# A planned order of work is drawn again: scatters ask later for their turn, and chance decides near ties

## The chip, the cores and the metric

The kernel runs on one core of a Trainium2 chip. A core has five engines, each with its own queue of instructions that it works off in order: TensorE (PE in the profile, PEld for its weight loads), VectorE (DVE), ScalarE (ACT), GpSimd (POOL) and SyncE (SP), which here only issues transfers. Engines wait for each other by semaphores. The metric is the device time of one execution in microseconds. Before the change it was 1603.57 us, the median of seven runs between 1598.36 and 1611.09.

## The reference

The input is x, 128 sequences of 32 tokens of width 256, and a context of 257 rows of width 256 for each sequence. Two layers are computed, each an addition to x after a layernorm:

```python
x = x + L0_xattn(layernorm(x), ctx)   # one head, all 257 context rows
x = x + L0_attn(layernorm(x))         # causal over the 32 tokens, one head of 128
x = x + L0_ffn(layernorm(x))          # 256 -> 1024 -> 256, ternary weights, 8-bit activations
x = x + L1_xattn(layernorm(x), ctx)   # 16 heads of 16
x = x + L1_attn(layernorm(x))         # five neighbours of each token
x = x + L1_ffn(layernorm(x))          # 8 experts 256 -> 1024 -> 256, two per token, with a capacity
```

For the last step each token's two best experts are found, the tokens are put into the experts' slots, each expert computes its slots, and the results are added to x, weighted by the two gates. A token that finds its expert full gets nothing from it.

## The kernel before

The 4096 tokens are 32 groups of 128 tokens (four sequences). A group goes through the first five steps and the choice of experts in `router` (L1123) as one thread of work; six groups are under way at a time, each in a lane of buffers. At the end of `router` the group's x is stored to the output and its normed rows to a table in HBM, each by one transfer that POOL issues (L1125 and L1128). After some groups a round of routing (`route`, L1166) finds ranks and slots for their tokens, and scatters token numbers and gates into a table of slots.

The experts' work is cut into 72 tiles of 128 slots (`expert_tile`, L1396). For each tile POOL issues four gathers (L1149): the first and second weight matrix of the expert (1 MB each, `w`, `kT` or `kn` by the buffer that is free), the slots' token numbers and gates (`ids`), and the tokens' rows (`xt`). PE turns the rows (L1433), does the two products (L373, with `xTm` and with `hT`), ACT does gelu between them (L1455), and ACT or DVE multiplies by the gate into `y` (L1474, L1475). Then POOL issues a scatter that adds `y` to the output (L1154). There are two buffers for `y`, and each is given back only when its scatter is done. The tiles of the early rounds run among the groups; some two dozen are left when the last group is through, and make the tail of the kernel.

The order of the instructions is not written by hand. Class `Order` (L80 to L229) is a small planner that runs while the kernel is built. Every thread is a generator that yields what it needs next: a buffer from a set (`Slots`), a pause in nanoseconds, another thread's end, or a list with an engine, a length in nanoseconds and the function that emits the instructions. `go_on` (L128) advances a thread until it asks for an engine, and puts it among the ready ones. `run` (L186) takes, again and again, the ready step that could begin first by the planner's own clock; among equal ones the thread's rank decides, which is mostly the number of the group. The emitted order is what each engine's queue then holds on the chip. In places where the planner foresees PE idle for at least 220 ns and little work in the time just before, `idle` (L477) puts in fillers, matmuls of the identity and a matrix of ones whose result nobody reads.

Three locks, each a set with one item, keep the planner from ordering transfers to the same table side by side: `at_slots`, `at_rows` and `at_out`. `locked` (L1141) is what takes them. It is called by the 72 scatters of `y` and the 32 stores of x with `at_out`, by the stores of normed rows with `at_rows`, and by the scatters of token numbers with `at_slots`; two transfers that clear spare rows of the output also use `at_out`. A thread gets the lock, then pauses for `EARLY`, 2500 ns, so that the data is surely there when POOL comes to the instruction, then asks for the engine, and gives the lock back when the planner's time for the landing, `LAND`, 4000 ns, is over. For a scatter of `y` that takes POOL for 1620 ns of the planner's time, so the lock is held for 2500 + 1620 + 4000 = 8120 ns. These numbers are the planner's, not measured ones.

Of the kernel before, what the change touches and what calls it, by code (L numbers as in the profile page):

```python
# [1 line left out]

# [66 lines left out]
class Slots:  # L69


    def __init__(self, items):
        self.free = [(0.0, i, t) for i, t in enumerate(items)]
        self.waiting = []
# [10 lines left out]
class Order:  # L85
# [5 lines left out]

    LAG = {"PE": 300.0, "DVE": 130.0, "ACT": 150.0, "POOL": 90.0, "SP": 3500.0}
    TABLE = 1300.0
    SWITCH = 1000.0
# [1 line left out]

    def __init__(self):
        self.until = dict.fromkeys(self.LAG, 0.0)  # L100
        self.idle = lambda ns: None
        self.recent = []
        self.array = 0.0
        self.ready = []
        self.table = None
        self.parts = None
        self.now = None
# [20 lines left out]
    def go_on(self, t, value):  # L128

        while True:  # L130
            try:
                ask = t.work.send(value)
            except StopIteration:
                t.done = t.at
                for w in t.waiting:
                    w.at = max(w.at, t.at)
                    outer, self.now = self.now, w
                    self.go_on(w, None)
                    self.now = outer
                return  # L140
            value = None
            if isinstance(ask, Slots):
                if not ask.free:
                    ask.waiting.append(t)
                    return
                best = min(ask.free, key=lambda f: f[:2])
                ask.free.remove(best)
                t.at = max(t.at, best[0])
                value = best[2]
            elif isinstance(ask, float):  # L150
                t.at += ask
            elif not isinstance(ask, list):
                if ask.done is None:
                    ask.waiting.append(t)
                    return
                t.at = max(t.at, ask.done)
            else:
                t.ask = ask
                self.ready.append(t)
                return  # L160

# [24 lines left out]
    def run(self):  # L186
        while self.ready:
            best = None
            for t in self.ready:
                for choice in t.ask:  # L190
                    begin = max(t.at, self.until[choice[0]])
                    ns = choice[1]
                    if choice[0] != "PE" and len(choice) > 3 and choice[3] and choice[3] != self.table:
                        ns += self.TABLE
                        begin += self.SWITCH
                    elif choice[0] == "PE" and self.divided(choice) != self.parts:
                        ns += self.DIVIDE if self.divided(choice) else self.WHOLE
                        begin += self.UNDIVIDED if self.divided(choice) else self.UNWHOLE
                    key = (begin, t.rank, begin + ns)
                    if best is None or key < best[0]:  # L200
                        best = (key, t, choice, ns)

            t = best[1]
            choice, ns = best[2], best[3]
            if len(t.ask) > 1:
                ends = [max(t.at, self.until[c[0]]) + c[1] + self.SPARE.get(c[0], 0.0) for c in t.ask]
                choice = t.ask[ends.index(min(ends))]
                ns = choice[1]
            self.ready.remove(t)
            if choice[0] == "PE":  # L210
                if self.divided(choice) != self.parts:
                    ns = choice[1] + (self.DIVIDE if self.divided(choice) else self.WHOLE)
                self.parts = self.divided(choice)
            elif len(choice) > 3 and choice[3]:
                self.table = choice[3]
            begin = max(t.at, self.until[choice[0]])
            if choice[0] == "PE":
                self.keep_busy(begin)
            array = self.array
            choice[2]()  # L220
            if choice[0] == "PE":
                self.recent.append((begin, begin + ns, self.array - array))
            self.until[choice[0]] = begin + ns
            t.at = begin + ns + (choice[4] if len(choice) > 4 else self.LAG[choice[0]])
            t.ask = None
            outer, self.now = self.now, t
            self.go_on(t, None)
            self.now = outer
        self.span = max(self.until.values())  # L229
# [3 lines left out]
def perceiver(ctx: ExitStack, tc: tile.TileContext, a: dict, out: bass.AP):  # L233
# [163 lines left out]
    at_slots, at_rows, at_out = (Slots([None]) for _ in range(3))  # L397
# [123 lines left out]
    def transfer(kb, emit):  # L521
        return [("SP", max(450.0, 1024 * kb / RATE), emit, None, 0.0)]

    def load_context(bs, got):

        kTs, kns = [], []
        for b in bs:
            kTs.append((yield from taken_from(keysT)))
            yield transfer(257, lambda: nc.sync.dma_start(kTs[-1][0], a["ctxT"][b]))
        for b in bs:  # L530
            kns.append((yield from taken_from(keys)))
            yield transfer(256, lambda: nc.sync.dma_start(kns[-1][0], a["ctx"][b]))
        got += zip(kTs, kns)
# [589 lines left out]
    def router(g, ln):  # L1123
        xg = ln.x
        sent = [order.thread(locked(at_out, "POOL", 1000, lambda: nc.gpsimd.dma_start(out[g * P : (g + 1) * P, :], xg)), order.now.rank)]  # L1125
        xn = yield from layernorm(ln, xg)
        sent.append(
            order.thread(locked(at_rows, "POOL", 1000, lambda: nc.gpsimd.dma_start(x_rows[g * P : (g + 1) * P, :], xn)), order.now.rank)  # L1128
        )
        xT = yield from transposed(ln, xn, "xnT")  # L1130
        ps = yield ps_g
        yield pe(430, lambda: products(ps[:, 0:E], [(xT[:, kc, :], wr[:, kc, :]) for kc in range(2)]))
        yield dve(75, lambda: nc.vector.tensor_copy(logits[:, g, :], ps[:, 0:E]))
        order.give(ps_g, ps)
        for t in sent:
            yield t

    EARLY = 2500.0
    LAND = 4000.0

    def locked(lock, engine, ns, emit):  # L1141

        yield lock
        yield EARLY
        yield [(engine, ns, emit, None, LAND)]
        order.give(lock, None)

# [18 lines left out]
    def route(r):  # L1166
# [103 lines left out]
        for i in range(RB):  # L1270
            for k in range(2):
                yield from locked(
                    at_slots, "POOL", 1000, lambda: scatter(slot_ids, islot[:, k, i : i + 1], ids[:, k, i, :])
                )
# [208 lines left out]
    def loads(*pairs):  # L1483
        for dst, src in pairs:
# [3 lines left out]
            yield transfer(n / 1024, lambda: nc.sync.dma_start(dst, src))  # L1488
        yield order.LAG["SP"]

# [172 lines left out]
    def load_one(b, kv):  # L1663
        yield from load_context([b], kv)
        yield order.LAG["SP"]

# [146 lines left out]
```

## Time and profile before

| what | value |
|---|---|
| median of seven runs | 1603.57 us |
| profiled execution | 1614.34 us, of which span 1612.6 us |
| mean granted clock of TensorE | 0.973 of full speed |
| matmuls on PE | 93% of the span busy |
| ACT, DVE, POOL | 62%, 61%, 48% busy |
| moved by DMA | 336.39 MB, 209 GB/s in the mean |
| the scatters of `y` | 72, POOL busy 1.63 us for each, from 422.7 us to the end |

The span runs from the first to the last instruction. Busy time counts instructions that compute or, on POOL, issue a transfer; waiting is not busy. A row of a timeline gives the start, the length, the engine, the line in the kernel, the operation, what is written and read, how many were merged into the row, and in brackets how long the engine was idle before it and who ended that. One matmul of 32-bit numbers in the program is two records in the trace.

### The profile page before, as it was taken

Reading aid. Unit: us, or ns where it says so; the run is one execution under the profiler, and the core shown is the slowest. Engines: PE = TensorE matmul, PEld = TensorE weight load, DVE = VectorE, ACT = ScalarE, POOL = GpSimd, SP = SyncE. Lnnn points to the kernel's source line nnn. Section 1 sums busy time; section 2 is a strip of 40 time slices with the busy share of each in tenths; the row PEclk is TensorE's granted clock in tenths of the full one; section 3 lists DMA queues with packets and bytes.
Section 4 is the critical chain, followed back from the end, with each engine's and each line's share of the span. In section 5 each row is a group of like instructions: output and inputs, shape, how many; then the busy total and the mean of one; then the engine's idle time right before and its main releaser. Section 6 shows DMA issues by size and latency. Waiting matters only on the chain. (4 is left out here: it accounts for less than half of the span.)

```text
span 1612.6 us, 43426 instructions
## 1 busy us (share of the span) xinstructions
PE 1494.6 (93%) x16758; PEld 1234.2 (77%) x16758; DVE 984.8 (61%) x3547; ACT 1003.3 (62%) x2654; POOL 775.4 (48%) x1025
## 2 busy tenths in 40 slices
PE   7889889798899999999999999999999999999997
PEld 6666666567667787887888788778877788888897
DVE  3777768887977777668566865777766744320000
ACT  1467756676767767777777676868777665322221
POOL 3412213344245555444445546445544556677763
PEclk8999989899999999999999999999999999999999
DMA  8673356356246676666666666757574367789996
GB/s 299 200 240 118 102 162 210 94 165 227 77 150 239 205 272 194 224 195 212 232 211 229 216 218 232 243 179 240 166 253 163 127 207 235 243 272 303 293 309 188
DMA packets 133150, 336.39 MB, mean 209 GB/s; under 512 B 17744, under 2 KB 43344, under 8 KB 114256
## 3 DMA queue, kind: packets, MB, share of 16 engines
q0 software_dynamic: 41984, 179.40, 34.2%
q1 hardware_dynamic: 90816, 154.09, 29.5%
q8 instruction: 132, 2.16, 0.6%
q14 instruction: 74, 0.61, 0.1%
q10 hardware_dynamic: 144, 0.13, 0.0%
HBM read 309.68 MB, written 23.87 MB: 207 GB/s over the span
## 5 line engine op out<-in xcount | busy, mean ns | idle before, releaser
L990 ACT ACTIVATE probs<-sps,nm 128x256 f32<-128x256 f32 x512 | 240.5, 485 | 44.1 <-DVE nm L946 35.3
L545 POOL TENSOR_SCALAR rstd<-mv 128x1 f32<-128x1 f32 x192 | 49.9, 260 | 427.1 <-DVE mv L540 344.2
L373 PE MATMUL ps<-w,hT 128*128 128x256 f32 x832 | 219.8, 389 | 2.8 <-DVE mx L707 1.4
L373 PE MATMUL ps<-xTm,w 128*128 128x128 f32 x1504 | 202.6, 278 | 0.9 <-ACT wide L509 0.4
L373 PEld LDWEIGHTS ps<-xTm,w 128*128 128x128 f32 x1504 | 190.0, 192 | 14.6 <-issue 3.6
L608 PE MATMUL sps<-ident,probs 128*128 128x128 f32 x1024 | 155.9, 287 | 18.4 <-ACT probs L990 16.0
L944 DVE TENSOR_REDUCE nm<-sps 128x2 f32<-128x512 f32 x256 | 164.0, 683 | 13.9 <-PE sps L373 13.9
L373 PEld LDWEIGHTS ps<-w,hT 128*128 128x128 f32 x832 | 147.2, 193 | 27.9 <-issue 7.6
L509 ACT COPY probsT<-sps 128x512 f32<-128x512 f32 x242 | 138.8, 595 | 46.3 <-PE sps L608 44.4
L1455 ACT ACTIVATE hT<-ps 128x512 f32<-128x512 f32 x144 | 85.4, 597 | 130.9 <-PE ps L373 128.6
L608 PEld LDWEIGHTS sps<-ident,probs 128*128 128x128 f32 x1024 | 122.9, 148 | 39.0 <-ACT probs L990 30.9
L1149 POOL DMA_INDIRECT w<-in_w_moe,i_exp x99 | 100.9, 1019 | 99.3 <-PE ps L373 59.4
L1154 POOL DMA_INDIRECT out<-y,ids x72 | 117.1, 1627 | 52.2 <-issue 25.3
L546 POOL TENSOR_TENSOR rstd<-rstd,mhalf 128x1 f32<-128x1 f32 x192 | 112.1, 584 | 16.1
L509 ACT COPY xnT<-ps 128x256 f32<-128x256 f32 x174 | 64.2, 376 | 80.6 <-PE ps L560 75.8
L990 ACT ACTIVATION_READ_ACCUMULATOR probs<-sps,nm 128x1 f32 x512 | 110.1, 215 | 0.0
L549 DVE TENSOR_SCALAR xn<-x,mv,rstd 128x256 f32<-128x256 f32 x173 | 73.6, 425 | 45.6 <-POOL rstd L546 44.3
L1154 POOL DMA_INDIRECT slot_ids<-tok_ids,islot x64 | 67.2, 1050 | 52.5 <-DMA slot_ids<-tok_ids,islot 20.4
L560 PE MATMUL ps<-ident,xn 128*128 128x128 f32 x384 | 76.1, 286 | 17.1 <-DVE xn L549 6.8
L373 PEld LDWEIGHTS sps<-probsT,kn 128*32 128x32 f32 x4096 | 67.3, 112 | 27.8 <-issue 16.3
L373 PE MATMUL sps<-probsT,kn 128*32 128x64 f32 x4096 | 85.6, 225 | 2.9 <-ACT probsT L509 2.6
L1475 ACT ACTIVATE y<-ps,ids 128x256 f32<-128x256 f32 x71 | 33.7, 475 | 85.5 <-PE ps L373 58.2
(304 smaller groups left out, 3531.5 us busy)
## 6 DMA issues: line engine op xcount, KB each, us to landing
kT<-in_ctxT SPq DMA_DIRECT2D x256, 257.0 KB
kn<-in_ctx SPq DMA_DIRECT2D x256, 256.0 KB
x<-in_x SPq DMA_DIRECT2D x32, 128.0 KB
last<-in_ctx_last SPq DMA_DIRECT2D x32, 128.0 KB
out<-x POOLq DMA_DIRECT2D x32, 128.0 KB
x_rows<-xn POOLq DMA_DIRECT2D x32, 128.0 KB
x_rows<-nothing SPq DMA_DIRECT2D x7, 512.0 KB
w<-in_w SPq DMA_DIRECT2D x2, 1024.0 KB
```

Source lines behind the costliest of these rows:

```text
L373: nc.tensor.matmul(out, lhsT=lhsT, rhs=rhs, **how)
L509: ("ACT", 60 + 0.815 * n, lambda: nc.scalar.copy(out, in_)),
L545: nc.gpsimd.tensor_scalar(rstd, mv[:, 1:2], EPS, None, ALU.add)
L546: nc.gpsimd.tensor_tensor(rstd, rstd, mhalf, ALU.pow)
L549: yield either(326, 1250, lambda e: e.tensor_scalar(xn, xg, mv[:, 0:1], rstd, ALU.subtract, ALU.mult))
L560: nc.tensor.transpose(pt[:, c, :], x[:, c * P : (c + 1) * P], ident)
L608: nc.tensor.transpose(by_key[:, i, c, :], e[:, i * LK + c * P : i * LK + (c + 1) * P], ident)
L944: nc.vector.tensor_reduce(nm[:, :, r], sps[r].rearrange("p (j k) -> p j k", j=2), AX.X, ALU.max)
L990: lambda: nc.scalar.activation(e[:, (2 * i + j) * LK : (2 * i + j + 1) * LK], sps[r][:, j * LK : (j + 1) * LK], AF.Exp, bias=nm[:, j, r : ...
L1149: nc.gpsimd.indirect_dma_start(out=dst, out_offset=None, in_=src, in_offset=bass.IndirectOffsetOnAxis(ap=idx, axis=0))
L1154: nc.gpsimd.indirect_dma_start(out=dst, out_offset=bass.IndirectOffsetOnAxis(ap=idx, axis=0), in_=src, in_offset=None, compute_op=op)
L1455: yield act(495, lambda: nc.scalar.activation(hT[:, 4 * half : 4 * half + 4, :].rearrange("p f t -> p (f t)"), hps, AF.Gelu), "gelu")
```

## The change

Three edits. The first is in `locked`: for `at_out` alone, the pause `EARLY` now comes ahead of the lock, so a scatter or a store of x waits out its slack while another holds the lock, and the planner holds the lock 2500 ns shorter. The other two are in the planner. Each time a thread asks for an engine, it gets a `late` between 0 and 80 ns from a random generator with a fixed seed, and `run` adds it to the time at which the step could begin when it compares the ready steps. The time at which the planner then lets the step begin is as before. With the fixed seed the order is the same in each build.

```diff
+    SEED, NOISE = 92, 80.0
...
     def __init__(self):
         self.until = dict.fromkeys(self.LAG, 0.0)
+        self.chance = random.Random(self.SEED)
...
                 t.ask = ask
+                t.late = self.NOISE * self.chance.random()
                 self.ready.append(t)
                 return
...
                 for choice in t.ask:
-                    begin = max(t.at, self.until[choice[0]])
+                    begin = max(t.at + t.late, self.until[choice[0]])
...
     def locked(lock, engine, ns, emit):
 
-        yield lock
-        yield EARLY
+        if lock is at_out:
+            yield EARLY
+            yield lock
+        else:
+            yield lock
+            yield EARLY
         yield [(engine, ns, emit, None, LAND)]
         order.give(lock, None)
```

## The prediction

> **What bounds the kernel now.** I read the page first, then busy time by stage, then the waits of the last stage, then single rows in order of time. The profiled execution took 1614.34 us (span 1612.6 us and 1.7 us around it), 10.8 us above the median of the seven runs, 1603.57 us. I make the sum against 1614.34 and carry the difference over to the median.
>
> ```profile
> PE 1494.6 (93%) x16758; PEld 1234.2 (77%) x16758; DVE 984.8 (61%) x3547; ACT 1003.3 (62%) x2654; POOL 775.4 (48%) x1025
> ```
>
> TensorE has work for 93% of the span. No instruction of real work is added or removed by this change, so time can only move where PE is idle, slow or doing filler. The second view is busy time by stage (after the length: PE, PEld, DVE, ACT, POOL, each with its count, then granted clock, DMA share, GB/s).
>
> ```profile
> 0.00:520.00 520.00, 448.40 (x5596) 339.65 (x5597) 387.35 (x1342) 324.35 (x953) 177.04 (x320) 0.94 0.54 174
> 520.00:1080.00 560.00, 544.85 (x6481) 453.73 (x6480) 390.31 (x1396) 412.25 (x1069) 280.61 (x367) 0.99 0.68 221
> 1080.00:1360.00 280.00, 267.96 (x3101) 225.59 (x3100) 178.09 (x654) 196.67 (x497) 153.46 (x183) 0.99 0.61 197
> 1360.00:1412.00 52.00, 50.66 (x360) 46.04 (x359) 19.17 (x103) 19.32 (x36) 34.40 (x40) 1.00 0.72 225
> 1412.00:1525.00 113.00, 105.27 (x705) 97.20 (x705) 9.85 (x56) 29.81 (x57) 81.17 (x76) 0.98 0.89 288
> 1525.00:1612.00 87.00, 77.42 (x526) 71.96 (x524) 0.00 (x0) 20.92 (x42) 48.73 (x43) 0.98 0.82 257
> ```
>
> Read the first number after the length: PE idles 71.6 us up to 520, 27.2 us from there to 1360 (15.1 and 12.0), and in the tail of expert tiles 1.3 and 7.7 us; the last 9.6 us are mostly the final scatter and the end. The tail is where the scatters matter. Its rows in order of time (start, length, engine, line, in brackets the idle time before and who ended it):
>
> ```profile
> 1482.57 1.62 POOL L1154 DMA_INDIRECT out<-y,ids  x1 [0.30 <-ACT hT L1455]
> ...
> 1490.86 0.47 ACT L1475 ACTIVATE y<-ps,ids 128x256 f32<-128x256 f32 x1 [2.41 <-DMA out<-y,ids]
> ...
> 1491.39 1.13 PE L373 MATMUL ps<-kT,hT 128*128 128x256 f32 x4 [0.77 <-ACT y L1475]
> 1491.48 0.61 ACT L1455 ACTIVATE hT<-ps 128x512 f32<-128x512 f32 x1
> 1491.55 1.61 POOL L1154 DMA_INDIRECT out<-y,ids  x1 [2.33 <-ACT y L1475]
> ...
> 1498.50 1.60 POOL L1154 DMA_INDIRECT out<-y,ids  x1 [0.30 <-issue]
> ...
> 1510.73 1.13 PE L373 MATMUL ps<-xTm,kT 128*128 128x128 f32 x8 [2.50 <-DMA kT<-in_w_moe,i_exp]
> 1511.70 1.43 PE L373 MATMUL ps<-w,hT 128*128 128x256 f32 x4
> 1512.93 1.92 PE L373 MATMUL ps<-xTm,kT 128*128 128x128 f32 x8
> 1514.63 1.51 PE L373 MATMUL ps<-w,hT 128*128 128x256 f32 x4
> 1515.98 1.06 PE L373 MATMUL ps<-xTm,kT 128*128 128x128 f32 x8
> ```
>
> This is one story. The y scattered at 1482.57 was begun at 1472.71 and ended at 1473.19: the scatter stood 9.4 us behind its result. It let go of its buffer 8.3 us after its start (the y two tiles on waits for it until 1490.86). Two y buffers turn over in two tiles, and a PE tile takes 4 x 0.89 + 4 x 0.865 + 0.22 = 7.24 us here (rows of 8, 4 and 2 matmuls between neighbours), so 14.5 us; 9.4 + 8.3 = 17.7 is too long. The next y is late, PE waits 0.77, POOL stands 2.33 in front of a scatter with weight gathers behind it, and two tiles later PE waits 2.50 us for weights and then runs slow until about 1516. POOL cannot catch up: from 1491.55 to 1498.50 a scatter and four gathers stand back to back and take 6.95 us of every 7.24.
>
> **The change part by part.** The order in which both programs were built can be compared without a run.
>
> *The scatters.* In the tail of before, a scatter of tile k stands behind the second weight gather of tile k+3 (30 scatters) and late on behind the row gather of k+5; in the changed order, for the last 22 full steps, behind those of k+2 and mostly k+4. One POOL instruction of 1.6 us moves ahead of two gathers of 1.25 us (0.95 and a gap of 0.30): 2.5 us earlier, so a lag of 6.9 and a turnover of 15.2 instead of 17.7 us. What it adds: the scatter meets its wait for y earlier, and behind it on POOL are the gathers of two weights, ids and rows. Hidden while the lag stays positive; it was 4.2 to 9.4 us from 1467 to 1597. The waits the story explains are, in the tail, kT 3.1, kn 1.2 and y 0.8 us, and 1.8 us of slow rows (1.43 for 1.03, 1.92 for 1.05, 1.51 for 1.03): 6.9. Ends: all PE waits of the tail (9.8) and the slow rows, a gain of 11.6; or five scatters that each hold POOL 2.5 us too early, less the 0.29 us that POOL has spare in each of 24 tiles, a loss of 5.5. I take -7, since the lag left is nearer to the rows with slack. The 32 stores of the groups' x go through the same function; each is one POOL instruction of 0.66 us that no PE step waits for: 0.
>
> *The fillers.* Both programs put matmuls of ones into foreseen idle time of PE. Before has 65, of which 24 (48 rows) stand between 1382 and 1429; the changed order has 44, none there.
>
> ```profile
> 1382.41 1.81 PE L373 MATMUL sps<-ident,ones 128*128 128x128 f32 x14
> 1384.05 0.38 PE L560 MATMUL ps<-ident,xn 128*128 128x128 f32 x2
> 1384.27 0.61 PE L373 MATMUL sps<-ident,ones 128*128 128x128 f32 x4
> ```
>
> No wait follows here: the next real step was ready and stood behind 1.64 and 0.62 us of filler. With the groups at 1386, 1397, 1425 and 1427 (0.40, 0.22, 0.68, 0.67) that is 4.2 us; a last group of 14 is followed by a wait of 2.27 us and costs nothing. I take -4, ends -4.2 and +1.8: with the filler gone the wait at 1425 may be 2.27 + 1.6 = 3.9 us, and the row at 1510 shows what follows a wait of 2.50 us, matmuls that lose 1.8 us; the granted clock from 1500 to 1520 is 0.91. One rule speaks against this part. The Trainium skill (TensorE: Matmul & The Clock Gate, Part 1) says that an idle window of about 3.4 us halves the clock, and by its figures a window at half clock would cost 1.7 us, an estimate near the trace's, though the trace's threshold lies lower.
>
> *The chance.* Up to 80 ns on a step's readiness changes who goes first, and from there on the whole order. Three things can be counted. (a) Changes between matmuls of the whole array and of parts of it: 438 before, 468 after. From 701.86 two rows of 0.112 take 0.32 until the first matmul on parts, and coming back eight take 1.00 instead of 0.89: 0.1 us each, 30 x 0.1 = +3 (0 if they fall into idle time, 4.5 at half as much again). (b) The first loads: the second folding weight is now the fifth load of SP, not the third, behind two x tiles of 128 KB; at 298 GB/s (first 40 us) +0.9 us. The weights now interleaved with the first group's context put its last keys at about 5.0 MB / 298 GB/s = 17 us and 2 to 3 for landing; they are used at 21.61: hidden, 2 us to spare. (c) Steps whose chain from the last PE product, at mean row lengths, is longer than the PE work ordered between: 113 with 35.7 us short before, 132 with 42.8 after (24.1 to 26.0 in the stage to 520; 9.0 to 13.9 to 1360). That is 7 us more, but chains explain only 36 of 108 us of idle PE; the rest is waiting behind other work on ACT and DVE, which the order alone doesn't price. Scaled to the real idle time it would be 5.6 + 14.8 + 1.5 = 22. On the other side the idle share that chains don't explain could fall by a tenth of its 72 us, -7. Fillers outside the tail, 41 and 44, say that the planner foresees as much idle time as before. I take 0, ends -7 and +22.
>
> Sum: -7 - 4 + 3 + 1 + 0 = -7, so 1614.3 - 7 = 1607.3 us profiled, and 1603.57 - 7 = 1596.6, say 1597 us.
>
> **Rivals.** *Same time.* The tail is as much DMA as PE: share 0.89 and 288 GB/s up to 1525, and 24 tiles instead of 23 follow the last routing. If weights arrive no sooner, -7 becomes 0 and fillers pay for mode changes: -4 + 3 + 1 = 0, 1604. Against it: the rows above show a late issue, not a slow transfer. *Slower by the groups' stages.* The tighter chains between 520 and 1360 cost what the scaling says, +14.8: -7 + 14.8 = +8, 1611. It decides from 7 us of idle PE added there. For it: 36 tight steps become 52; against: DVE and ACT are at 70 and 74% from 520 to 1080, so queues are not full, and another ready step usually covers. *Slower by blocked gathers.* Scatters wait at POOL's head for y: +5.5 for -7, -4 + 3 + 1 + 5.5 = 5.5, 1609; from three such waits on. Against: lags of 4 to 9 us. That the order isn't changed as said is excluded by the built order.
>
> **How the numbers follow.** Forecast 0.50, same time 0.20, groups' stages 0.21, blocked gathers 0.09. About 0.3% (4.8 us) is what a measurement can tell from no change. The forecast's own range, 1583 to 1602, has a sixteenth within that bound; same time gives most of its chance to it: faster 0.49, same 0.21, slower 0.30. Range: 1603.6 - 11.6 - 4.2 - 7 + 1 = 1582 below, and the two slower cases with a little over, 1614 above.
>
> **What would show it.** In the profile after: no filler between the last two routings; waits of y for the DMA of out gone from ACT in the tail, and scatters 4 to 7 us behind y; PE's waits for kT and kn in the tail under 2 us and no rows of 1.9 us. PE idle from 80 to 1360 within 5 us of 84; more means that the chance costs what I set to nothing. I am wrong if POOL waits for y ahead of many scatters, or if stages before 1360 shift by over 8 us either way.

## The result, and the profile after

The changed kernel takes 1612.74 us (median of 31 runs, 1607.22 to 1618.31), before 1605.06 us (73 runs, 1596.20 to 1615.53). The ratio is 1.0048, with a 95% interval of 1.0037 to 1.0060: **slower by 7.7 us**, where the forecast was faster by 7. It lies inside the range given, and near the rival that loses in the groups' stages (1611 us).

One caution first. The profiled execution of before was a long one (1614.34 us, 9 us over the median), that of the changed kernel (1613.55 us) is 0.8 us over its own. So the two pages show equally long kernels, and the loss can't be read from them by subtraction. Further down I use profiles of other kernels that hold before's order.

The page and the busy time by stage of the changed kernel (after the length: PE, PEld, DVE, ACT, POOL, then granted clock, DMA share, GB/s):

```profile
PE 1494.1 (93%) x16716; PEld 1228.2 (76%) x16716; DVE 992.1 (62%) x3566; ACT 997.6 (62%) x2637; POOL 774.0 (48%) x1024
```

```profile
0.00:520.00 520.00, 450.10 (x5537) 342.45 (x5538) 393.42 (x1351) 320.13 (x939) 167.62 (x312) 0.93 0.55 176
520.00:1080.00 560.00, 543.01 (x6481) 448.41 (x6483) 387.00 (x1364) 411.95 (x1068) 288.70 (x374) 1.00 0.66 214
1080.00:1360.00 280.00, 268.89 (x3153) 223.61 (x3146) 187.50 (x707) 196.97 (x497) 150.67 (x184) 1.00 0.62 205
1360.00:1412.00 52.00, 49.15 (x324) 45.88 (x323) 16.16 (x100) 18.68 (x35) 36.81 (x40) 0.93 0.76 242
1412.00:1525.00 113.00, 108.35 (x742) 100.78 (x741) 7.97 (x46) 30.37 (x60) 84.03 (x78) 1.00 0.92 295
1525.00:1612.00 87.00, 74.56 (x492) 67.07 (x491) 0.00 (x0) 19.52 (x40) 46.12 (x41) 0.97 0.78 249
```

PE is idle for 69.9 us up to 520, for 28.1 from there to 1360 and for 19.9 after that; before had 71.6, 27.2 and 18.6. Idle time alone shows next to nothing. The waits of PE in the tail, from 1410 on (us in total, times, longest):

```profile
PE ps L378 <- DMA kT<-in_w_moe,i_exp: 5.1, 5, 1.8
PE ps L378 <- DMA w<-in_w_moe,i_exp: 3.1, 4, 1.6
PE ps L378 <- DMA kn<-in_w_moe,i_exp: 0.3, 1, 0.3
```

and rows of that tail in order of time:

```profile
1513.72 0.47 ACT L1484 ACTIVATE y<-ps,ids 128x256 f32<-128x256 f32 x1 [0.26 <-DMA out<-y,ids]
1516.61 1.60 POOL L1163 DMA_INDIRECT out<-y,ids  x1 [2.03 <-DMA out<-y,ids]
...
1521.67 1.13 PE L378 MATMUL ps<-xTm,kT 128*128 128x128 f32 x8 [0.58 <-DMA kT<-in_w_moe,i_exp]
...
1532.46 1.61 POOL L1163 DMA_INDIRECT out<-y,ids  x1 [0.30 <-issue]
...
1540.75 1.60 POOL L1163 DMA_INDIRECT out<-y,ids  x1 [2.26 <-DMA out<-y,ids]
...
1549.53 1.13 PE L378 MATMUL ps<-xTm,kT 128*128 128x128 f32 x8 [1.83 <-DMA kT<-in_w_moe,i_exp]
```

While weights are still being gathered, the wait that the prediction wanted away is nearly away: ACT waits 0.26 us for a buffer of `y` here, and again 2.02 us at 1591.98, after the last gather; before had 2.41 us at 1490.86, and PE's 0.77 us behind it are gone. What remains is on POOL. The scatter at 1540.75 was held up for 2.26 us, and not by its own data: what ended its wait is a transfer `out<-y`, the scatter issued before it at 1532.46, 8.3 us earlier. A scatter does not start before the one ahead of it has landed: in seven profiles (before, the changed kernel twice, and four kernels of the experiments) each of the 104 transfers to `out` on POOL but the first starts at least 0.28 us after the landing of the one before it, taken from the last update of that transfer's semaphore in the trace.

That wait is not new. In before's tail the prediction's own rows show it, with the row of one more `y`:

```profile
1482.72 0.47 ACT L1475 ACTIVATE y<-ps,ids 128x256 f32<-128x256 f32 x1 [0.26 <-PE ps L373]
```

This is the `y` after the one that ended at 1473.19, so it is what the scatter at 1491.55 adds to the output. It had been ready for 8.4 us. POOL's 2.33 us in front of that scatter were not for a late `y`, as the prediction read them, but for the landing of the scatter of 1482.57, the same event that let ACT go on at 1490.86. The weight gathers stand behind the waiting scatter on POOL, and PE, which waited 6.6 us for weights and rows in before's tail, now waits 8.5.

**Where the time goes, at equal work.** To compare kernels of different order I priced each kind of matmul with its mean distance to the next in before's trace, left the fillers out, and read off when TensorE had done 5, 40 and 85% of this work. In each cell: length of the stretch, in brackets the idle time of PE (up to its last matmul), and the time lost to the clock (half the length of the stretches in which the trace grants 0.5 instead of 1.0), all in us. All rows are single profiles, from chips where before takes 1603 to 1605 us. The cuts depend on the prices: other ways to price the same work move them by several us, and the loss between 5 and 40% then comes out between 12 and 25 us.

| kernel | to 5% | 5 to 40% | 40 to 85% | 85% to the end |
|---|---|---|---|---|
| before | 124 (22.2; 8.5) | 576 (53.9; 25.6) | 654 (22.7; 5.1) | 259 (9.8; 4.1) |
| before's order up to the tail (`lock_tail_2`, below) | 123 (21.5; 8.5) | 574 (55.4; 20.5) | 652 (23.2; 3.4) | 262 (15.5; 3.3) |
| changed kernel | 115 (16.5; 8.5) | 590 (60.9; 29.0) | 648 (20.6; 0.0) | 259 (11.6; 6.2) |
| changed kernel, second profile | 114 (15.8; 8.5) | 594 (60.6; 34.1) | 649 (21.0; 0.0) | 259 (13.4; 4.5) |
| chance alone | 116 (15.6; 10.2) | 596 (64.4; 30.7) | 648 (23.5; 1.7) | 259 (7.0; 5.9) |

The change gains 8 to 10 us in the first stretch, loses 14 to 20 us between 5 and 40% of the work (about 115 to 705 us), gains 3 to 6 after that, and is within 3 us in the last. Three parts of the loss can be counted. PE idles 5 to 7 us more. By the table's measure 8 to 14 us more are lost at half clock against `lock_tail_2`, and 3 to 9 against before's own profile. That measure is an upper bound, since PE is idle in part of the half-clock windows; with half of PE's busy time in them it is 4 to 9 us against `lock_tail_2` and -1 to +4 against before. Two profiles of one order differ by 5 us here. Fillers, 20 records in this stretch instead of 2, are worth 2.5 us. The rest stays open.

Which part of the change does it? The three profiles with chance all lose in this stretch. The two with the lock edit and no chance (`lock_head`, among the groups only, and `lock_only_2`, everywhere, both below) lose nothing there: however the work is priced, they need 3 to 7 us less for it than `lock_tail_2`.

### The profile page after: what moved, and what is told of

Its sections match the earlier page's. It is cut to its first block, busy times and chain, and to the rows that moved or that the text cites. A ratio compares the mean times of both kernels' runs of the same rounds, so it can differ in the third digit from the quotient of the medians.

```text
span 1611.8 us, 43335 instructions
## 1 busy us (share of the span) xinstructions
PE 1494.1 (93%) x16716; PEld 1228.2 (76%) x16716; DVE 992.1 (62%) x3566; ACT 997.6 (62%) x2637; POOL 774.0 (48%) x1024
## 5 line engine op out<-in xcount | busy, mean ns | idle before, releaser
L378 PEld LDWEIGHTS ps<-xTm,w 128*128 128x128 f32 x1568 | 199.7, 192 | 20.4 <-ACT hT L1464 4.0
L378 PE MATMUL ps<-xTm,w 128*128 128x128 f32 x1568 | 210.7, 278 | 4.5 <-DMA w<-in_w_moe,i_exp 3.1
L378 PE MATMUL ps<-w,hT 128*128 128x256 f32 x784 | 207.6, 389 | 0.3
L378 PEld LDWEIGHTS ps<-w,hT 128*128 128x128 f32 x784 | 136.1, 191 | 25.9 <-issue 8.9
L378 PEld LDWEIGHTS sps<-probsT,kn 128*32 128x32 f32 x4096 | 66.5, 110 | 25.0 <-issue 13.1
L1158 POOL DMA_INDIRECT ids<-slot_ids,i_row x72 | 72.6, 1008 | 24.0 <-issue 17.2
```

Source lines behind the costliest of these rows:

```text
L378: nc.tensor.matmul(out, lhsT=lhsT, rhs=rhs, **how)
L1158: nc.gpsimd.indirect_dma_start(out=dst, out_offset=None, in_=src, in_offset=bass.IndirectOffsetOnAxis(ap=idx, axis=0))
```

## The experiments

Some kernels ran on chips where before itself takes 1671 to 1672 us, others where it takes 1603 to 1605 as in the first comparison, and a few on both; every ratio is taken against runs of before on the same chip.

| kernel | ratio, before at 1603 to 1605 us | ratio, before at 1671 to 1672 us |
|---|---|---|
| the whole change | 1.0048 [1.0037, 1.0060] and 1.0047 [1.0029, 1.0066] | 0.9959 [0.9934, 0.9985] and 0.9931 [0.9904, 0.9958] |
| chance alone | 1.0101 [1.0073, 1.0128] | 1.0171 [1.0125, 1.0217] |
| lock edit alone | 1.0084 [1.0056, 1.0112] | 1.0053 [1.0021, 1.0085] |
| lock edit among the groups only | 1.0039 [1.0019, 1.0060] | |
| lock edit in the tail only | 1.0030 [1.0010, 1.0050] | 0.9987 [0.9968, 1.0005] |
| the whole change, tail's scatters as before | 1.0058 [1.0041, 1.0075] | |

### The two parts, each alone

Chance alone is the changed kernel with `locked` as in before:

```diff
-        if lock is at_out:
-            yield EARLY
-            yield lock
-        else:
-            yield lock
-            yield EARLY
+        yield lock
+        yield EARLY
```

The lock edit alone is the changed kernel with no chance:

```diff
-    SEED, NOISE = 92, 80.0
+    SEED, NOISE = 92, 0.0
```

> The chance with the same seed, the lock as before. Theory A: as slow as the whole change or slower, 1.003 to 1.007, from the groups' stages: their chains are 26.8 + 16.5 us short in this order against 24.1 + 9.0 in before. Theory B: 0.998 to 1.002. Since any difference draws another order from then on, an order of its own kind is expected, not half of the change.

> The change without its chance: the pause ahead of the lock for the output's transfers, and the spread of the chance set to 0. Theory A (the chance costs, the lock is innocent): ratio 0.996 to 1.001, at most 1 us slower, since mode changes of the array are 428 against 438 and the scatters stand one gather earlier. Theory B (the lock costs: scatters that stand earlier hold up the gathers behind them): 1.003 to 1.006, and in the profile POOL waits for y in front of scatters of the tail, with PE waits for kT, kn and w above before's 4.3 us. In both its last 28 fillers stay.

> The kernel before, unchanged. Every theory expects a ratio of 1 within 0.15%. It is run for its profile: the profile shown of before is one execution of 1614.34 us, 0.6% above its own median of 1605.06, while that of after (1611.8 us span) lies at its median. If the profiled execution of before was a slow one, a second one is near 1605 us and shows where the first lost its 8 us: I expect 5 us or more of it in rows of matmuls at a low granted clock before 520 us and the rest in the tail. If instead profiling itself costs before 8 us, the second is near 1613 as well.

On a chip with before at 1671 us: chance 1702.15 us, lock 1680.98, before unchanged 1672.56 (1.0001, 0.9969 to 1.0033). Both parts lose, chance most.

> The chance without the lock edit, again. It was the dearest part, 1.0171. If that is its order and not the chip, 1.015 to 1.02 again; on a chip where before takes about 1605 us, where the prediction was made, its cost should shrink with that of before's own stalls, to 1.005 to 1.01.

> The lock edit without chance, again, beside the complement. If its cost comes from the redrawn groups' stages on any chip: 1.005 again, +8 to +9 us. If it belonged to the chip of that call: within 0.2% of before here.

On a chip with before at 1604.25 us: chance 1620.29 us, lock 1616.91. With the intervals above that is +16 us (12 to 21) and +13 us (9 to 18). Together, in the changed kernel, they cost +7.5 us and not +29: each redraws the whole order, and the lock edit on top of the chance gives 7 us back (1620.29 to 1613.14). So the 7.5 us can't be divided between the parts.

### The whole change again

> The whole change, unchanged, so that it stands beside the others on one chip: 1.003 to 1.007 if it does as in its own measurement (1.0048); above 1.01 if a chip with slower transfers punishes its order more, as the order of the chance alone was punished (1.017).

> The whole change once more. The first comparison gave 1.0048 and the second, on a chip where before itself takes 1672 us, 0.9959. If the sign belongs to the chip, this follows the time of before here: slower by 0.5% where before takes about 1605 us, faster by 0.4% where it takes about 1671 us.

> The whole change beside its two parts on one chip. Where before takes about 1605 us: slower by 0.5% as in the first comparison. Where before takes about 1671 us: faster by 0.4 to 0.7%, as in the second and third. Anything else would mean that the sign does not go with the chip's pace.

1666.37 us against 1672.35, 1661.42 against 1672.03, and 1613.14 against 1604.25. The sign goes with the chip: on two chips where before needs 4% more time the same change is faster by 0.4 and 0.7%; in two comparisons where before takes 1604 to 1605 us it is slower by 0.5%. On the slower chips the stretch between 5 and 40% of the work again loses 20 us (580 us for before unchanged, 601 and 603 for the changed kernel), but from 85% to the end before unchanged needs 285 us and the changed kernel 268 and 269. That the tail decides the sign is likely, but not shown: the profiled execution of before unchanged (1662.13 us) is the fastest of its twelve, 10 us under their median, so these three profiles do not themselves show the gain.

### Other draws

The whole change with another seed (1, and 3):

```diff
-    SEED, NOISE = 92, 80.0
+    SEED, NOISE = 1, 80.0
```

The whole change without chance for the steps of SP:

```diff
-                t.late = self.NOISE * self.chance.random()
+                t.late = self.NOISE * self.chance.random() * (ask[0][0] != "SP")
```

Chance alone, and only for the first 120 us of the planner's time:

```diff
-                t.late = self.NOISE * self.chance.random()
+                t.late = self.NOISE * self.chance.random() * (t.at < 120000.0)
```

> The whole change with seed 1 in place of 92. Theory D (the order of before is an unusually good one of its kind, and any redrawn order loses, whichever part of the change redraws it): 1.003 to 1.015. Theory A in the narrow sense (seed 92 is an unlucky draw): 0.995 to 1.002. Its order has 454 mode changes and chains 44.1 us short, both worse than before's 438 and 35.7.

> The same with seed 3. Theory D: 1.003 to 1.015 again. Seed 92 unlucky: around 1. Were counted tight chains a measure of time, seeds 1 (44.1) and 3 (42.1) would both lie at or just behind seed 92 (42.8).

> The whole change, but steps on SP get no chance, so that the loads keep their order by rank from the start: wq and wk first, then the first group's context, then the other weights, as in before. Theory C (the interleaved loads of the start and of the context later are what costs): 0.998 to 1.001, 5 us or more better than the whole change, and PE reaches the first choice of experts no later than before. Theory A: the chance among the steps of the computing engines still costs, 1.003 to 1.006.

> Before with the changed kernel's chance only for steps that are ready in the first 120 us of the planner's time, and the lock as before: the first loads and the first two groups are ordered as in the changed kernel, which had 9 us more of its work done at 120 us than before; no step is drawn by chance after that, though the order differs from before's for good. If the gain at the start is one to keep, and the later loss comes from chance in the groups' stages: about -9 us, a ratio of 0.995. If any change of order in the groups' stages costs what the lock alone did (+9 us) the ratio is 1.00, and if what is gained at the start only makes the groups meet later waits earlier, 1.00 as well, with the lead gone by 500 us.

All with before at 1671 to 1672 us: seed 1 gives 1684.20 us, 1.0076 (1.0048 to 1.0104); seed 3 gives 1698.93 us, 1.0177 (1.0137 to 1.0217); without chance for SP 1683.20 us, 1.0071 (1.0040 to 1.0102); chance at the start only 1679.12 us, 1.0035 (1.0014 to 1.0055). Seed 92 is by far the best of three draws. The lead at the start is the interleaved first loads': with chance at the start the first 5% of the work take 112 us, without chance for SP's steps, which leaves before's first loads, 125 us. It isn't kept: with chance at the start, 5 to 40% take 600 us, as in the changed kernel, though no step was drawn by chance after 120 us. So what costs there seems to be a redrawn order, not chance as such.

### The clock between 5 and 40% of the work

The busy time from 120 to 560 us in three profiles: before's order (the kernel with the lock edit in the tail only, equal to before up to there), the changed kernel (its second profile) and chance alone; the clock is the third number from the end.

```profile
120.00:560.00 440.00, 387.17 (x5116) 296.94 (x5130) 344.17 (x1215) 301.18 (x894) 159.06 (x254) 0.95 0.50 162
```

```profile
120.00:560.00 440.00, 384.31 (x4863) 291.51 (x4860) 333.29 (x1155) 285.64 (x849) 149.38 (x235) 0.92 0.49 157
```

```profile
120.00:560.00 440.00, 384.28 (x4918) 291.24 (x4919) 337.04 (x1168) 289.48 (x856) 150.40 (x238) 0.93 0.49 158
```

PE is busy for nearly as long, and does less: 4863 matmuls instead of 5116. A clock lower by 0.03 over 440 us is 13 us; before's own profile (0.94, 5100 matmuls) and the first one of the changed kernel (0.93, 4951) lie closer together. How a low clock comes about is seen in windows of 3.4 us of the changed kernel, cut where its granted clock changes, with the row of PE that follows the wait:

```profile
277.70:281.10 3.40, 1.10 (x10) 0.98 (x8) 3.06 (x16) 1.61 (x3) 1.40 (x3) 1.00 0.11 39
281.10:284.50 3.40, 2.22 (x32) 1.26 (x32) 3.26 (x12) 2.99 (x6) 0.62 (x2) 0.50 0.00 0
284.50:287.90 3.40, 3.40 (x54) 1.72 (x40) 3.19 (x14) 0.19 (x1) 2.30 (x4) 0.50 0.66 186
287.90:291.30 3.40, 3.40 (x20) 3.28 (x16) 2.09 (x10) 0.39 (x1) 0.96 (x2) 0.50 0.69 199
291.30:294.80 3.50, 3.31 (x15) 2.16 (x14) 2.25 (x9) 3.25 (x13) 0.00 (x0) 0.50 0.36 121
294.80:298.20 3.40, 3.13 (x30) 2.76 (x28) 2.36 (x13) 2.20 (x8) 0.00 (x0) 1.00 0.00 0
```

```profile
282.28 2.71 PE L378 MATMUL sps<-kT,wide 32*64 32x256 f32 x32 [3.48 <-ACT wide L889]
```

The first window holds 1.10 us of work; the next four are granted half the clock, though the last three are full or nearly so. One wait of 3.48 us for ACT (`wide`) thus costs about 6 us more (half of the 12.3 us that PE works in these four windows). The planner's fillers are meant against this: `keep_busy` adds them where, by the planner's clock, less than half of the last 3400 ns was work. None stands in front of this wait, and the planner prices a matmul the same whatever the clock.

The clock of the trace changes in steps of 3.41 us. In the three profiles above, between 100 and 1400 us, 26 windows had more than 1.7 us of idle PE, and 23 of them were followed by a window at half clock; of 43 windows with 1.0 to 1.4 us it was 10. The Trainium skill (TensorE: Matmul & The Clock Gate, Part 1) puts the limit at an idle gap of about 3.4 us; by that rule only the longest waits of these profiles, 3.48 and 3.49 us, would count. The measurement decides: in this kernel a window that is half empty is nearly always enough.

### The scatters in the tail

The prediction's largest term, by itself: the order is before's, instruction for instruction, until the last two dozen tiles, and there a scatter asks earlier. A second kernel, the complement, has `<` in the place of `>`.

```diff
-        yield lock
-        yield EARLY
+        if lock is at_out and order.now.at > 1360000.0:
+            yield EARLY
+            yield lock
+        else:
+            yield lock
+            yield EARLY
```

> Before, with the pause ahead of the lock only for the scatters of the last two dozen tiles and no chance anywhere: the order is before's, instruction for instruction, until the tail, the fillers are all there, and in the tail a scatter stands behind the second weight gather of tile k+2 and the row gather of k+4 instead of k+3 and k+5. This is the prediction's step of the scatters alone. The prediction: -7 us, a ratio of 0.9956, and fewer waits for weights in the tail. Rival, the tail is paced by what the transfers move (2.4 MB for a tile): the ratio is 1.000 within 2 us, and the spacing of tiles after the last routing is that of before. Rival, scatters now block the gathers behind them: up to +5.5 us, 1.0034.

> Before's own order with the earlier scatters in the tail alone, again, where it was 0.9987 on a chip with before at 1672 us. By the difference of the two kernels with the lock edit on the chip with before at 1604 us it is now slower by 5 us, 1.003; by the prediction it is 0.9956. On a chip like the one of the first try it is again within 2 us of before.

1670.09 us against 1672.03 on one chip, 1608.59 against 1602.78 on the other: -2 us (-5 to +1) on the first, +5 us (+2 to +8) on the second. -7 us is excluded on both. The waits of PE in this tail on the second chip:

```profile
PE ps L1437 <- DMA xt<-x_rows,ids: 4.1, 3, 2.6
PE ps L373 <- DMA kT<-in_w_moe,i_exp: 4.0, 4, 1.7
PE ps L373 <- DMA kn<-in_w_moe,i_exp: 3.2, 2, 2.1
PE ps L373 <- DMA w<-in_w_moe,i_exp: 1.8, 1, 1.8
PE ps L373 <- ACT xTm L509: 1.1, 1, 1.1
```

That is 13.1 us for weights and rows, where before's order with late scatters had 6.6.

> The complement of the kernel with the tail's scatters alone: the pause ahead of the lock for the stores of x and for the scatters among the groups, not for the tail's scatters, and no chance. The prediction costed this part at 0. The lock edit everywhere cost 9 us (ratio 1.0053) and in the tail alone gained 2 (0.9987); if the parts add, this is slower by 11 us, 1.0065. If the tail's part depends on where the groups leave it, it lies between 1.000 and 1.005.

1611.78 us, +6 us (3 to 10). This kernel and the one with the lock edit everywhere, on the same chip, have one order up to the tail; their curves of work lie within 1 us of each other until 80%, and from 85% on one takes 266 and the other 277 us. By the medians the earlier scatters cost 5.1 us (1616.91 less 1611.78); the profiles exaggerate it, since the kernel with late scatters was caught in its fastest execution (1604.56 us). The term that the prediction put at 0, the lock edit among the groups, costs these 6 us by itself; where, that fast profile can't say. The waits of PE for weights and results from 1405 us on (a wait for rows of about 10 us, which both have, is left out), and those of POOL's scatters from 1420. First the kernel with late scatters, as in before:

```profile
PE ps L373 <- DMA kn<-in_w_moe,i_exp: 1.2, 1, 1.2
PE ps L373 <- ACT xTm L509: 0.4, 1, 0.4
```

```profile
POOL out L1158 <- issue: 15.1, 10, 5.0
POOL out L1158 <- ACT y L1479: 6.8, 6, 2.3
POOL out L1158 <- DMA out<-y,ids: 4.6, 2, 2.9
```

Then the kernel with early scatters:

```profile
PE ps L378 <- DMA kT<-in_w_moe,i_exp: 3.1, 1, 3.1
PE ps L378 <- DMA kn<-in_w_moe,i_exp: 3.0, 2, 1.8
PE ps L378 <- DMA w<-in_w_moe,i_exp: 1.5, 3, 0.8
PE ps L378 <- ACT hT L1464: 0.8, 1, 0.8
```

```profile
POOL out L1163 <- issue: 13.3, 15, 5.7
POOL out L1163 <- ACT y L1484: 12.7, 3, 5.9
POOL out L1163 <- DMA out<-y,ids: 11.0, 4, 4.0
```

PE waits 7.6 us for weights instead of 1.2. POOL's lines are to be read with care. With late scatters, in none of the six waits put down to ACT was it the scatter's own `y` that came last: that had been ready for 7 to 10 us. With early ones the three are for the scatter's own `y`, but they come at 1595 us and later, after the last weight gather, where nothing stands behind them. So I took the landings from the trace instead. The table counts the scatters between 1420 us and the last weight gather that stood at POOL's head until the one before them had landed, with POOL's idle time in brackets. PE's time is its waits for weights and rows in the tail (for the middle pair without the wait for rows of about 10 us).

| order | late scatters | early scatters |
|---|---|---|
| before's | 11 of 21 (15.3 us); PE 6.6 us | 11 of 21 (21.5 us); PE 13.1 us |
| lock edit among the groups | 9 of 19 (13.9 us); PE 1.2 us | 8 of 20 (15.6 us); PE 7.6 us |
| changed kernel (next run; two profiles with early ones) | 3 of 21 (6.9 us); PE 3.0 us | 7 and 8 of 22 (12.7 and 11.8 us); PE 8.5 and 12.2 us |

`lock_only_2` and the changed kernel have one more wait each in front of a scatter, of about 5 us, that neither the landing nor `y` explains. In each pair POOL stands longer at the scatters when they are early, and PE waits 5 to 9 us longer for what is gathered behind them. That is the rival of the blocked gathers, with the landing of the scatter before in the place of a late `y`.

> The whole change, but the scatters of the tail take the lock as in before: every instruction is the changed kernel's until the tail (47 of 72 scatters), and there a scatter stands behind the second weight gather of tile k+3 and the row gather of k+5 or k+6 instead of k+2 and k+4. On the chip where before took 1604 us, the lock edit everywhere without chance took 5 us more than the lock edit among the groups alone, so the earlier scatters of the tail cost 5 us there. If that holds in the changed kernel too: 5 us faster than it, about 1608 against before's 1604, a ratio of 1.002. If the prediction's term is right: 7 us slower than it, 1.009. If the tail's transfers set its pace whatever the scatters do: 1.0047.

The edit is the condition above with `<` in the changed kernel's `locked`. 1612.08 us against 1602.78: 1.0058 (1.0041 to 1.0075), against 1.0047 (1.0029 to 1.0066) with the early scatters. In the changed kernel they are thus worth -2 us (-6 to +2, the two intervals taken together). Both sides of the step are seen in the profiles. With late scatters ACT waits ten times for a buffer of `y`, up to 3.07 us, with early ones never or twice; PE idles 7.1 us from 85% to the end with late ones, 11.6 and 13.4 with early ones. What the step gives on ACT it takes on POOL. With the tail's scatters worth so little, and the last stretch of the table equal, the change loses its 7.7 us in the groups' stages.

### What paces the tail

In the changed kernel, late tiles leave out part of the second product:

```diff
                 for fc in range(f, f + 2):
+                    if late and 0 < fc < 7:
+                        order.array += P / 2.4 * 4 * D / P
+                        continue
```

> The whole change; in the expert tiles after the last groups, TensorE does two of the eight parts of the second product and leaves out six, 2.6 us of its 7.24 us in each tile (so those tiles' results are not the reference's). Order, transfers and all other work stay. If TensorE paces the tail, the spacing of tiles falls from 7.9 us towards 5.3 us and the kernel is 50 to 60 us shorter. If the transfers pace it (2.4 MB for a tile at the 295 to 311 GB/s that the tail showed are 7.7 to 8.1 us), the spacing stays at 7.5 to 8 us and the time falls by less than 10 us.

The time is 1650.37 us (one run) against 1661.42 for the changed kernel on that chip; 24 tiles with 2.6 us less would be 62. The distance of tiles goes from 8.33 to 7.92 us. The stretch from 1470 to 1630, whole (first) and with the work left out (second):

```profile
1470.00:1630.00 160.00, 150.07 (x996) 138.04 (x995) 0.00 (x0) 39.27 (x80) 107.77 (x100) 0.97 0.89 286
```

```profile
1470.00:1630.00 160.00, 113.67 (x769) 105.12 (x769) 0.00 (x0) 39.38 (x81) 110.04 (x101) 0.89 0.93 303
```

PE has 36 us less to do and waits instead. The transfers, and POOL that issues them, set the pace at nearly the same value as PE does, so that there was little for an earlier scatter to win in the tail. This is one execution, on a chip of the slower kind. (Part of the freed time went to a lower clock, 0.89.)

### The fillers

Before, without its last 24 fillers:

```diff
-        for i in range(n):
+        for i in range(n if order.until["PE"] < 1.1e6 else 0):
```

> The kernel before with its order kept, but the 24 fillers after the second but last routing left out. The prediction counted 4 us for them: 0.9974, 0.9965 to 0.9985. If PE merely waits in their place, 1.000; if the clock falls in the longer wait, up to 1.001.

1668.92 us against 1672.35, a ratio of 0.9989 (0.9963 to 1.0016): -2 us, between -6 and +3, on a slower chip. The predicted -4 is neither shown nor excluded.

## Why the prediction failed, point by point

- **What bounds the kernel**: it held that time can only move where PE is idle, slow or at filler. But the sum priced idle time by stage, and the clock only in the tail (slow rows, fillers). Between 120 and 560 us before already ran at 0.94 to 0.95, and what a new order does to that share was not in any term.
- **The chance, (c): taken at 0, ends -7 and +22. This is the step that failed.** By itself it costs 16 us (12 to 21). The stretch from 5 to 40% of the work, 115 to 705 us, grew by 14 to 20 us. The scaling of idle time gave 5.6 us for the stage up to 520, which is the right size for the idle part (5 to 7 us), and nothing for the half-clock windows that follow (up to 9 us by PE's busy time in them, up to 14 by their length). It put its 14.8 us into 520 to 1360, where nothing was lost: idle 27.2 before, 28.1 after. The argument for 0, that another ready step usually covers, holds in that later stage, and not in the early one.
- **The lock edit among the groups: taken at 0, 6 us (3 to 10) without chance.** The reason given, that no PE step waits for a store of x, leaves out that the edit redraws everything behind it, as the chance does. What it costs on top of the chance is not known.
- **The scatters: taken at -7, measured +5 in before's order (+2 to +8; on the slower chip -2, -5 to +1), and -2 (-6 to +2) in the changed one.** The mechanism was half right: ACT's waits for a `y` buffer went while weights were gathered, all but 0.26 us. The sentence that failed is "Hidden while the lag stays positive". A scatter also waits for the landing of the scatter ahead of it, 8.3 us after that one's start at 1532.46, and moving it in the queue does not move that. It waits at POOL's head instead, with the gathers behind it. The row at 1491.55 showed this wait in before and was read as a late `y`. The sum was thin as well: its own turnover after the change, 15.2 us, was still more than the 14.5 that two tiles take. The rival had scatters that wait for `y`: while weights are gathered that happens twice at most in a tail.
- **The lag left**: 4 to 7 us were foreseen behind `y`, and the scatters stand 0.3 to 6 us behind it, 3 in the median. PE's waits for weights in the tail were to fall under 2 us and are 8.5.
- **The fillers: -4, not settled.** They are gone as foreseen, none between the last two routings.
- **The first loads: +1, in truth -8 to -10 us** at 5% of the work. I looked for the one weight that comes later and not at PE's idle time up to there, which falls from 22 to 16 us. At 15% of the work 2 to 5 us of the lead are left against before's profile, and none against `lock_tail_2`'s.
- **The mode changes: +3, not measured by themselves.** The stretch from 40 to 85% is 3 to 6 us shorter with more of them (220 instead of 196), so they don't show there; between 5 and 40%, with 220 instead of 203, they can't be told from the rest.
- **Rivals.** The time is that of the rival that loses in the groups' stages (1611 us), with the wrong stage; the 7 us of idle PE between 520 and 1360 from which it was to decide did not come. "Same time" had the right reason in part: the tail is paced by transfers too.
- **What would show it**: idle time from 80 to 1360 stayed within 5 us of 84 (86.7) and said nothing, since it cuts by time and not by work, and a lower clock is no idle time. The other sign, stages before 1360 that shift by over 8 us, did come.

## What to carry to other kernels

When a change redraws an order, count PE's windows at half clock as well as its idle time, stage by stage, before calling a redraw neutral: here the clock had a part in the loss that the sum had no term for, and the 0.94 of the first stage in the profile of before pointed at it. Before moving an instruction ahead in a queue, list everything it waits for; one that still waits for its predecessor's landing only carries its wait to the head of the queue, where others stand behind it. A draw among orders that differs by half a per cent has no sign of its own until it is measured on more than one chip. When a profile names the semaphore that ended a wait, check that the data named was not ready long before.

## What the runs showed of the hardware that I had not expected

- **Half a window of idle PE nearly always halves the clock for the next**: 23 of 26 windows of 3.41 us with over 1.7 us idle, and up to four such windows after one wait of 3.48 us.
- **The same program takes 4% longer on some chips**: before 1671 to 1672 us on three, 1603 to 1605 in the other comparisons. On the slower ones TensorE's signals come late. In the profile of before unchanged, 99 signals to other engines came more than 0.6 us after the modelled end of their matmul, 156 us in sum; in a profile from a faster chip there are at most two before the kernel's end, the longest 3.5 us. The rows of one such place:

```profile
1462.81 0.44 PE L1433 MATMUL ps<-ident,xt 128*128 128x128 f32 x2 [1.58 <-DMA xt<-x_rows,ids]
...
1470.58 0.37 ACT L509 COPY xTm<-ps 128x256 f32<-128x256 f32 x1 [10.61 <-remote]
...
1471.01 1.22 PE L373 MATMUL ps<-xTm,w 128*128 128x128 f32 x4 [7.09 <-issue]
```

  ACT copies what the transposes at 1462.81 leave, but the signal for it is recorded at 1470.50, 7.3 us after they should have ended, and PE waits 7.09 us for the copy. The weight gathers land no later on these chips (after 1360 us, the last landing signal of a gather comes 6.1 us after its issue in the median for before unchanged, against 7.3 in the trace of before), so these transfers don't explain it. What delays TensorE there stays open; so does why the changed kernel's tail is the shorter one there.
